# A graph layer's edge loop: folding and adding the group sums later, in own PSUM banks, with the edge attributes copied into PSUM by ScalarE

## The chip, the cores and the metric

The kernel runs on one core of a Trainium2 chip. The time is device microseconds of one launch; a lower one is better.

## The reference

It is a graph layer with 6250 nodes, 206250 edges (sorted by their target `dst`) and 64 features, all in fp32:

```python
h = jnp.maximum(_layernorm(x, axis=-1), 0.0)
msg = jax.nn.relu(h[src] + edge_attr)                      # per edge
agg = jax.ops.segment_sum(msg, dst, num_segments=6250)
z = h + agg
out = x + jax.nn.relu(z @ W1 + b1) @ W2 + b2
```

## The kernel before

**Data.** The edges are taken in groups of 1024, 8 for each of the 128 partitions: 201 full groups and a short one of 4 columns (`NG` is 201, `G` is 8). `z` is kept in SBUF with features on partitions and nodes along the free side. The normalised rows `h` are also written to HBM as `h_rows`, from which edges gather. Groups 0 to 3 (`RAW`) gather from `x` itself and are normalised edge by edge in `norm_edges` (L147 to L157), so that gathers can start before `h_rows` is there.

**Loading.** `load(g)` issues one 256 KB DMA of edge attributes (`ea`) on SyncE's queue and eight gathers (`xg`) on GpSimd's queue (L130), each an indirect DMA of 128 rows. Both tiles have 12 buffers (`LOOK`).

**One group.** `window_sum(g)` builds a one-hot matrix of the edges' targets within a window of 64 nodes on VectorE (`oh`, L294), adds `xg` and `ea` into a PSUM tile `full` (L299, VectorE), and splits the Relu of it into three bf16 parts whose sum is the fp32 value: Relu on ScalarE (L301), the rest on VectorE (L302), its cast on ScalarE (L304), the last rest on VectorE (L305). Eight matmuls (L308) of one-hot and parts add up in the PSUM tile `agg`, 64 targets by three parts.

**Behind it.** `turn(g)` folds the three parts on VectorE (L278) and transposes the sum on TensorE (L280) into PSUM; `sum_into_z(g)` adds it to 64 columns of `z` (L285), at a place that is read from `dst` into VectorE's registers, eight groups at a time (L265). In the loop, group g's `window_sum` is followed by the turn of g-1 and the z add of g-2 (`LAG`).

**Blocks.** When no later group can reach a block of 512 nodes (`READY`), `hidden(c)` multiplies it by W1 (L316) with bias and Relu on ScalarE (L318); one group later `result(c)` multiplies by W2 (L326), adds `x` and `b2` on VectorE (L328) and stores it from SyncE's queue (L330). There are 12 blocks and a short one.

**Once.** Ahead of the loop, the node layernorm (L164 to L200) and `slot`, each edge's place in its window (L219). After group 8, `find_left` checks with three VectorE passes over 128x1612 (L240 to L242), a reduce (L245) and some small ones (L254 to L258) that every edge fell into its window; if one did not, a slow path would follow at the end. After group 9, 13 VectorE adds put b2 into `x_sb` (L353, L355).

The order on each engine is the order of the code: nothing is rescheduled, and engines run ahead of each other as far as buffers and semaphores let them.

Of the kernel before, what the change touches and what calls it, by code (L numbers as in the profile page):

```python
# [9 lines left out]
F32 = mybir.dt.float32  # L10
# [3 lines left out]
ALU = mybir.AluOpType  # L14
# [3 lines left out]
N, E, D = 6250, 206250, 64  # L18
P = 128
G = 8  # L20
GE = P * G
NG = E // GE
# [6 lines left out]
CT = TJ + 1  # L29
W = 64  # L30
WB = 512
R = 4
NB = N // (P * R)
TN = N - NB * P * R
XC = 3
EPS = 1e-5
LOOK = 12
LAG = 2
RV = 8
RAW = 4  # L40
READY = [min(NG, -(-E * P * R * (c + 1) // (N * GE)) + 1) for c in range(NB)]
# [4 lines left out]
def kernel(  # L46
# [14 lines left out]
    nc = tc.nc  # L61
# [5 lines left out]
    work = ctx.enter_context(tc.tile_pool(name="work", bufs=4))  # L67
    dram = ctx.enter_context(tc.tile_pool(name="dram", bufs=1, space=bass.MemoryType.DRAM))
    psum = ctx.enter_context(tc.tile_pool(name="psum", bufs=2, space=bass.MemoryType.PSUM))
# [6 lines left out]
    for c in range(0, NB, XC):  # L76
        nc.sync.dma_start(
            out=x_sb[:, c:c + XC].rearrange("p b r d -> p b (r d)"),
# [55 lines left out]
    def load(g):  # L134
        ea = edge.tile([P, G, D], F32, name="ea")
        attr_load(ea, g)
        xg = edge.tile([P, G, D], F32, name="xg")
        gather(xg, src_sb[:, cols_of(g)], G if g < NG else CT, x if g < RAW else h_rows)
        return ea, xg
# [4 lines left out]
    loaded = [load(g) for g in range(RAW)]  # L144
# [57 lines left out]
    heads, rows = [], []  # L202
# [10 lines left out]

    base = const.tile([1, NG + 1], F32, name="base")
    nc.vector.tensor_copy(base, dst_sb[0:1, 0:C + 1:G])
    pb = psum.tile([P, R * D], F32, name="out", bufs=1)
    nc.tensor.matmul(pb[:, :NG + 1], ones[0:1, :], base, start=True, stop=True)
    slot = const.tile([P, C + CT], F32, name="slot")
    nc.vector.scalar_tensor_tensor(  # L219
# [15 lines left out]

    left = const.tile([P, C + CT], F32, name="left")
    flag = const.tile([1, 1], I32, name="flag")

    def find_left():
        nc.vector.tensor_scalar(left, slot, 1.0, None, op0=ALU.is_lt)  # L240
        nc.vector.scalar_tensor_tensor(left, slot, float(W), left, op0=ALU.is_gt, op1=ALU.add)
        nc.vector.scalar_tensor_tensor(left, dst_sb, 1.0, left, op0=ALU.add, op1=ALU.mult)  # L242
        nc.vector.memset(left[:TD, C + TJ:], 0.0)
        most = const.tile([P, 1], F32, name="most")
        nc.vector.tensor_reduce(most, left, AX.X, ALU.max)  # L245
        pf = psum.tile([P, R * D], F32, name="out", bufs=1)
        nc.tensor.matmul(pf[0:1, 0:1], most, ones[:, 0:1], start=True, stop=True)

        done = const.tile([1, NG + 1], F32, name="done")
        for c in range(-1, NB):  # L250
            to = READY[c + 1] + 1 if c + 1 < NB else NG + 1
            fr = READY[c] + 1 if c >= 0 else 0
            if fr < to:
                nc.vector.memset(done[:, fr:to], float(P * R * (c + 1)))  # L254
        nc.vector.tensor_tensor(done, base, done, ALU.is_lt)
        late = const.tile([1, 1], F32, name="late")
        nc.vector.tensor_reduce(late, done, AX.X, ALU.max)
        nc.vector.tensor_tensor(flag, late, pf[0:1, 0:1], ALU.add)  # L258
# [12 lines left out]
    aggs = {}  # L271

    turned = {}

    def turn(g):
        pa = aggs.pop(g)
        rows = work.tile([W, D], F32, name="agg_rows")
        nc.vector.tensor_reduce(rows, pa.rearrange("w t d -> w d t"), AX.X, ALU.add)  # L278
        pt = psum.tile([D, W], F32, name="turned", bufs=1)
        nc.tensor.transpose(pt, rows, ident[:W, :W])  # L280
        turned[g] = pt

    def sum_into_z(g):
        at = window_start(g)
        nc.vector.tensor_tensor(z[:, ds(at, W)], z[:, ds(at, W)], turned.pop(g), ALU.add)  # L285

    def window_sum(g):
        n = G if g < NG else CT
        cols = cols_of(g)
        ea, xg = loaded[g] if g < RAW else load(g)  # L290
        if g < RAW:
            norm_edges(xg)
        oh = work.tile([P, G, W], BF16, name="oh")
        nc.vector.tensor_tensor(  # L294
            oh[:, :n], slot[:, cols].unsqueeze(2).to_broadcast([P, n, W]),
            wslots.unsqueeze(1).to_broadcast([P, n, W]), ALU.is_equal)

        full = psum.tile([P, G, D], F32, name="full", bufs=2)
        nc.vector.tensor_tensor(full[:, :n], xg[:, :n], ea[:, :n], ALU.add)  # L299
        parts = work.tile([P, G, 3, D], BF16, name="parts")  # L300
        nc.scalar.activation(parts[:, :n, 0, :], full[:, :n], AF.Relu)  # L301
        nc.vector.scalar_tensor_tensor(full[:, :n], full[:, :n], 0.0, parts[:, :n, 0, :],  # L302
                                       op0=ALU.max, op1=ALU.subtract)
        nc.scalar.copy(parts[:, :n, 1, :], full[:, :n])  # L304
        nc.vector.tensor_tensor(parts[:, :n, 2, :], full[:, :n], parts[:, :n, 1, :], ALU.subtract)  # L305
        pa = psum.tile([W, 3, D], F32, name="agg", bufs=2)
        for j in range(n):
            nc.tensor.matmul(pa, oh[:, j, :], parts[:, j], start=(j == 0), stop=(j == n - 1))  # L308
        aggs[g] = pa


    def hidden(c):
        n0 = c * P * R
        p, r = (P, R) if c < NB else (TN, 1)
        p1 = psum.tile([D, P * R], F32, name="big", bufs=1)
        nc.tensor.matmul(p1[:, :p * r], w1_sb, z[:, n0:n0 + p * r], start=True, stop=True)  # L316
        h1 = work.tile([D, R, P], F32, name="h1")
        nc.scalar.activation(h1[:, :r, :p], p1[:, :p * r].rearrange("d (p r) -> d r p", r=r), AF.Relu, bias=b1_sb)  # L318
        return h1

    def result(c, h1):
        n0 = c * P * R
        p, r = (P, R) if c < NB else (TN, 1)
        p2 = psum.tile([P, R * D], F32, name="out", bufs=1)
        for k in range(r):
            nc.tensor.matmul(p2[:p, k * D:(k + 1) * D], h1[:, k, :p], w2_sb, start=True, stop=True)  # L326
        o = work.tile([P, R, D], F32, name="o")
        nc.vector.tensor_tensor(o[:p, :r].rearrange("p r d -> p (r d)"), p2[:p, :r * D],  # L328
                                x_sb[:p, c, :r].rearrange("p r d -> p (r d)"), ALU.add)
        nc.sync.dma_start(out=out[n0:n0 + p * r, :].rearrange("(p r) d -> p (r d)", r=r),  # L330
                          in_=o[:p, :r].rearrange("p r d -> p (r d)"))

    hid = {}

    def blocks_behind(g):
        for c in sorted(hid):
            result(c, hid.pop(c))
        for c in range(NB):
            if READY[c] == g:
                hid[c] = hidden(c)  # L340

    for g in range(NG + 1):
        window_sum(g)
        if g >= 1:
            turn(g - 1)
        if g >= LAG:
            sum_into_z(g - LAG)
            blocks_behind(g - LAG)
        if g == 8:
            find_left()  # L350
        if g == 9:
            for c in range(NB):
                nc.vector.tensor_tensor(x_sb[:, c], x_sb[:, c],  # L353
                                        b2_sb.unsqueeze(1).to_broadcast([P, R, D]), ALU.add)
            nc.vector.tensor_tensor(x_sb[:TN, NB, 0, :], x_sb[:TN, NB, 0, :], b2_sb[:TN], ALU.add)  # L355
    sum_into_z(NG + 1 - LAG)
    blocks_behind(NG + 1 - LAG)
    turn(NG)
    for g in range(NG + 2 - LAG, NG + 1):
        sum_into_z(g)  # L360
        blocks_behind(g)
    hid[NB] = hidden(NB)
    for c in sorted(hid):
        result(c, hid.pop(c))


    def all_windows(msg, lf, n):
# [12 lines left out]
    with tc.If(any_left > 0):  # L380
        with tc.For_i(0, NG, 1) as i:
            idx = work.tile([P, G], I32, name="idx")
            lf = work.tile([P, G], F32, name="lf")
            nc.vector.tensor_copy(idx, src_sb[:, ds(i * G, G)])
            nc.vector.tensor_copy(lf, left[:, ds(i * G, G)])
            ea = edge.tile([P, G, D], F32, name="ea")
            nc.sync.dma_start(out=ea.rearrange("p j d -> p (j d)"),
                              in_=edge_attr[ds(i * GE, GE), :].rearrange("(p j) d -> p (j d)", j=G))
            xg = edge.tile([P, G, D], F32, name="xg")
            gather(xg, idx, G, h_rows)  # L390
            all_windows(combine(xg, ea, G), lf, G)
        ea = edge.tile([P, G, D], F32, name="ea")
        attr_load(ea, NG)
        xg = edge.tile([P, G, D], F32, name="xg")
        gather(xg, src_sb[:, C:], CT, h_rows)
        all_windows(combine(xg, ea, CT), left[:, C:], CT)

        for c in range(NB + 1):
            result(c, hidden(c))


# [37 lines left out]
```

## Time and profile before

| | |
|---|---|
| timed runs, six | median 2051.39 us (2050.29 to 2052.81) |
| profiled execution | 2049.77 us, span 2048.0 us |
| busy share | GpSimd 75%, VectorE 33%, TensorE 20% (weight loads 14%), ScalarE 13% |
| gathers | 1612 (1580 from `h_rows`, 32 from `x`), median 944 ns each, from 4.8 us to 2030.4 us |
| attribute loads | 201 of 256 KB, median 4.8 us from issue to landing |
| the granted TensorE clock | 1.00 in every stage |

In the profile's timeline a line has the start and the length in us, the engine, the line of the kernel, the operation, the tile written and the tiles read (`out<-in`), and, in brackets, how long the engine had been idle and what ended that. In a table by stage a line has the stretch and its length, then for each of PE, PEld (weight loads), DVE (VectorE), ACT (ScalarE) and POOL (GpSimd) the busy time and the number of instructions, then the granted clock, the DMA engines' share and GB/s.

### The profile page before, as it was taken

To read this page: it belongs to the slowest core of one execution; us is meant where nothing else is said; L and a number is where in the kernel's file an instruction comes from. 1 tells how busy PE (TensorE), PEld (TensorE's weight loads), DVE (VectorE), ACT (ScalarE), POOL (GpSimd) and SP (SyncE) were. 2 spreads that over 40 slices of the span, in tenths; PEclk is the share of its full clock that TensorE was granted. 3 is DMA by queue.
4 is the path that set the end of the run, shared out by engine and by line. 5 is a ranking of instruction groups with operands and counts; after the bars stand their busy time and mean duration, and the time that the engine had idled before them with its cause. 6 is when DMAs were issued, how large, how long until landed. Compare 5 with 4: busy or idle time off the path is not lost.

```text
span 2048.0 us, 9645 instructions
## 1 busy us (share of the span) xinstructions
PE 409.7 (20%) x1991; PEld 287.2 (14%) x1991; DVE 670.7 (33%) x1321; ACT 269.2 (13%) x450; POOL 1535.9 (75%) x1619
## 2 busy tenths in 40 slices
PE   2121211211121121122121122112112112112212
PEld 1111111111111111111111111111111111111111
DVE  4662333333323333323333333333233332332332
ACT  3211111111111111111111111111111111111111
POOL 7777777777777777777777777777777777777774
DMA  5211221131131131131122113113113113211311
GB/s 179 62 38 27 84 53 27 44 99 27 26 111 26 26 106 37 27 96 42 27 80 62 27 26 112 26 27 111 32 26 101 37 27 96 47 27 26 104 26 23
DMA packets 87525, 112.95 MB, mean 55 GB/s; under 512 B 30948, under 2 KB 35684, under 8 KB 87460
## 3 DMA queue, kind: packets, MB, share of 16 engines
q0 software_dynamic: 51584, 52.93, 13.5%
q1 hardware_dynamic: 34628, 57.65, 8.3%
q10 hardware_dynamic: 1248, 1.70, 0.2%
q14 instruction: 48, 0.39, 0.1%
q8 instruction: 17, 0.28, 0.1%
HBM read 108.96 MB, written 3.20 MB: 55 GB/s over the span
## 4 chain that ended last, share of the span: by engine, by line
POOL 57%; issue 22%; DMA 17%; DVE 1%; ACT 1%; PE 1%; DVEq 0%; POOLq 0%; ACTq 0%
POOL xg L130 57%; DMA xg<-h_rows,src_sb 17%; PE big L196 0%; ACT z L197 0%; DMA ea<-in_edge_attr_dram 0%; DMA src_sb<-in_src_main_dram 0%; DVE full L302 0%; DVEq L265 0%; DVE x_sb L353 0%; DVE full L299 0%; ACT parts L301 0%; ACT parts L304 0%; DVE parts L305 0%; PE out L326 0%; PE big L316 0%
## 5 line engine op out<-in xcount | busy, mean ns | idle before, releaser
L130 POOL DMA_INDIRECT xg<-h_rows,src_sb x1580 | 1502.1, 951 | 481.5 <-issue 439.1
L308 PE MATMUL agg<-parts,oh 128*64 128x192 bf16 x1612 | 299.8, 367 | 1532.0 <-DVE parts L305 1532.0
L308 PEld LDWEIGHTS <-oh 128*64 128x64 bf16 x1612 | 230.0, 168 | 1586.4 <-DVE parts L305 1568.2
L299 DVE TENSOR_TENSOR full<-xg,ea 128x512 f32<-128x512 f32 x202 | 141.1, 698 | 929.7 <-DMA xg<-h_rows,src_sb 908.8
L301 ACT ACTIVATE parts<-full 128x512 bf16<-128x512 f32 x202 | 120.4, 596 | 1512.5 <-DVE full L299 1510.0
L302 DVE SCALAR_TENSOR_TENSOR full<-full,parts 128x512 f32<-128x512 f32 x202 | 141.1, 699 | 149.7 <-ACT parts L301 149.7
L305 DVE TENSOR_TENSOR parts<-full,parts 128x512 bf16<-128x512 f32 x202 | 139.4, 690 | 131.5 <-ACT parts L304 131.5
L304 ACT CAST parts<-full 128x512 bf16<-128x512 f32 x202 | 118.2, 585 | 154.6 <-DVE full L302 154.6
L294 DVE TENSOR_TENSOR oh<-slot,wslots 128x512 bf16<-128x512 f32 x202 | 135.3, 670 | 0.0
L280 PE MATMUL turned<-ident,agg_rows 64*64 64x64 f32 x202 | 63.1, 312 | 59.8 <-DVE z L285 59.0
L285 DVE TENSOR_TENSOR z<-z,turned 64x64 f32 x202 | 41.1, 203 | 87.6 <-issue 84.5
L278 DVE TENSOR_REDUCE agg_rows<-agg 64x64 f32<-64x192 f32 x202 | 68.4, 338 | 0.0
L280 PEld LDWEIGHTS turned<-ident,agg_rows 64*64 64x64 f32 x202 | 25.5, 126 | 117.4 <-DVE z L285 67.7
L130 POOL DMA_INDIRECT xg<-in_x_dram,src_sb x32 | 32.6, 1019 | 12.4 <-issue 9.4
L316 PE MATMUL big<-z,w_sb 64*64 64x512 f32 (+1 forms) x26 | 24.2, 1032 | 0.3 <-DVE z L285 0.3
L326 PE MATMUL out<-w_sb,h 64*128 64x64 f32 (+1 forms) x98 | 23.6, 418 | 1.2 <-ACT h L318 1.2
L326 PEld LDWEIGHTS out<-w_sb,h 64*128 64x128 f32 (+1 forms) x98 | 22.3, 329 | 3.2 <-ACT h L318 3.2
L196 PE MATMUL big<-ident,ln_h 128*64 128x128 f32 x48 | 12.7, 421 | 33.8 <-DVE ln_h L178 19.1
L328 DVE TENSOR_TENSOR o<-out,x_sb 128x256 f32<-128x256 f32 (+1 forms) x13 | 5.3, 409 | 37.9 <-PE out L326 37.9
L318 ACT ACTIVATE h<-big,b_sb 64x512 f32<-64x512 f32 (+1 forms) x13 | 8.5, 656 | 56.4 <-PE big L316 56.4
L197 ACT COPY z<-big 64x512 f32<-64x512 f32 x12 | 12.6, 1050 | 11.5 <-PE big L196 11.5
L196 PEld LDWEIGHTS big<-ident,ln_h 128*64 128x64 f32 x48 | 6.4, 159 | 39.6 <-issue 19.1
(52 smaller groups left out, 64.0 us busy)
## 6 DMA issues: line engine op xcount, KB each, us to landing
ea<-in_edge_attr_dram SPq DMA_DIRECT2D x201, 256.0 KB, 4.8
xg<-h_rows,src_sb POOLq DMA_INDIRECT x1580, 2.4
x_sb<-in_x_dram SPq DMA_DIRECT2D x4, 384.0 KB, 7.9
h_rows<-ln_h SPq DMA_DIRECT2D x4, 384.0 KB
out_dram<-o SPq DMA_DIRECT2D x12, 128.0 KB, 1.7
dst_sb<-in_dst_main_dram ACTq DMA_DIRECT2D x1, 804.0 KB
src_sb<-in_src_main_dram ACTq DMA_DIRECT2D x1, 788.0 KB
xg<-in_x_dram,src_sb POOLq DMA_INDIRECT x32, 3.0
```

The costliest lines, as they stand in the source:

```text
L130: nc.gpsimd.indirect_dma_start(out=xg[:, j, :], out_offset=None, in_=rows[:, :], in_offset=bass.IndirectOffsetOnAxis(ap=idx[:, j:j + 1], a ...
L278: nc.vector.tensor_reduce(rows, pa.rearrange("w t d -> w d t"), AX.X, ALU.add)
L280: nc.tensor.transpose(pt, rows, ident[:W, :W])
L285: nc.vector.tensor_tensor(z[:, ds(at, W)], z[:, ds(at, W)], turned.pop(g), ALU.add)
L294: nc.vector.tensor_tensor(oh[:, :n], slot[:, cols].unsqueeze(2).to_broadcast([P, n, W]), wslots.unsqueeze(1).to_broadcast([P, n, W]), ALU. ...
L299: nc.vector.tensor_tensor(full[:, :n], xg[:, :n], ea[:, :n], ALU.add)
L301: nc.scalar.activation(parts[:, :n, 0, :], full[:, :n], AF.Relu)
L302: nc.vector.scalar_tensor_tensor(full[:, :n], full[:, :n], 0.0, parts[:, :n, 0, :], op0=ALU.max, op1=ALU.subtract)
L304: nc.scalar.copy(parts[:, :n, 1, :], full[:, :n])
L305: nc.vector.tensor_tensor(parts[:, :n, 2, :], full[:, :n], parts[:, :n, 1, :], ALU.subtract)
L308: nc.tensor.matmul(pa, oh[:, j, :], parts[:, j], start=(j == 0), stop=(j == n - 1))
L326: nc.tensor.matmul(p2[:p, k * D:(k + 1) * D], h1[:, k, :p], w2_sb, start=True, stop=True)
```

## The change

ScalarE copies `ea` into `full`, one group ahead (`take(g+1)` at the head of `window_sum(g)`), and VectorE then adds `xg` to `full` in place. The turn stands two groups behind (`TLAG`), the z add six (`LAG`). `agg` holds two groups in one tile and `turned` four, each with two buffers. The block's products, the start's `pb` and `find_left`'s sum share one tile `big`; `result` and its output add and store are done in separate passes, two and four groups after `hidden`. The small steps at the end of `find_left` move to `judge`, after group 14, and the b2 adds to after group 15.

```diff
-LAG = 2
+LAG = 6
+TLAG = 2
+AB = 2
+TB = 4
...
-    pb = psum.tile([P, R * D], F32, name="out", bufs=1)
+    pb = psum.tile([P, R * D], F32, name="big", bufs=1)
...
+    def judge():
+        pf = found.pop("all")
...
     def turn(g):
         pa = aggs.pop(g)
-        rows = work.tile([W, D], F32, name="agg_rows")
+        rows = work.tile([W, D], F32, name="agg_rows", bufs=LAG)
         nc.vector.tensor_reduce(rows, pa.rearrange("w t d -> w d t"), AX.X, ALU.add)
-        pt = psum.tile([D, W], F32, name="turned", bufs=1)
+        if g % TB == 0:
+            turns.append(psum.tile([D, TB, W], F32, name="turned", bufs=2))
+        pt = turns[-1][:, g % TB]
         nc.tensor.transpose(pt, rows, ident[:W, :W])
         turned[g] = pt
...
+    def take(g):
+
+        n = G if g < NG else CT
+        ea, xg = loaded[g] if g < RAW else load(g)
+        full = psum.tile([P, G, D], F32, name="full", bufs=2)
+        nc.scalar.copy(full[:, :n], ea[:, :n])
+        taken[g] = full, xg
+
     def window_sum(g):
         n = G if g < NG else CT
         cols = cols_of(g)
-        ea, xg = loaded[g] if g < RAW else load(g)
+        if g + 1 <= NG:
+            take(g + 1)
+        full, xg = taken.pop(g)
...
-        full = psum.tile([P, G, D], F32, name="full", bufs=2)
-        nc.vector.tensor_tensor(full[:, :n], xg[:, :n], ea[:, :n], ALU.add)
+        nc.vector.tensor_tensor(full[:, :n], full[:, :n], xg[:, :n], ALU.add)
...
-        pa = psum.tile([W, 3, D], F32, name="agg", bufs=2)
+        if g % AB == 0:
+            banks.append(psum.tile([W, AB, 3, D], F32, name="agg", bufs=2))
+        pa = banks[-1][:, g % AB]
...
     def blocks_behind(g):
+        for c in sorted(res):
+            if READY[c] + 4 <= g:
+                store(c, res.pop(c))
         for c in sorted(hid):
-            result(c, hid.pop(c))
+            if READY[c] + 2 <= g and not res:
+                res[c] = result(c, hid.pop(c))
         for c in range(NB):
             if READY[c] == g:
                 hid[c] = hidden(c)
 
+    take(0)
     for g in range(NG + 1):
         window_sum(g)
-        if g >= 1:
-            turn(g - 1)
+        if g >= TLAG:
+            turn(g - TLAG)
         if g >= LAG:
             sum_into_z(g - LAG)
             blocks_behind(g - LAG)
         if g == 8:
             find_left()
-        if g == 9:
+        if g == 14:
+            judge()
+        if g == 15:
             for c in range(NB):
...
-    sum_into_z(NG + 1 - LAG)
-    blocks_behind(NG + 1 - LAG)
-    turn(NG)
-    for g in range(NG + 2 - LAG, NG + 1):
+    for g in range(NG + 1 - TLAG, NG + 1):
+        turn(g)
+    for g in range(NG + 1 - LAG, NG + 1):
         sum_into_z(g)
         blocks_behind(g)
     hid[NB] = hidden(NB)
+    for c in sorted(res):
+        store(c, res.pop(c))
     for c in sorted(hid):
-        result(c, hid.pop(c))
+        store(c, result(c, hid.pop(c)))
```

More of the change, by code (lines that the diff above doesn't have):

```diff
@@ L237 @@
     flag = const.tile([1, 1], I32, name="flag")
+    found = {}
     def find_left():
@@ L245, in find_left @@
         nc.vector.tensor_reduce(most, left, AX.X, ALU.max)
-        pf = psum.tile([P, R * D], F32, name="out", bufs=1)
+        pf = psum.tile([P, R * D], F32, name="big", bufs=1)
         nc.tensor.matmul(pf[0:1, 0:1], most, ones[:, 0:1], start=True, stop=True)
+        found["all"] = pf
+    def judge():
+        pf = found.pop("all")
         done = const.tile([1, NG + 1], F32, name="done")
@@ L273 @@
     turned = {}
+    banks = []
+    turns = []
     def turn(g):
         pa = aggs.pop(g)
-        rows = work.tile([W, D], F32, name="agg_rows")
+        rows = work.tile([W, D], F32, name="agg_rows", bufs=LAG)
         nc.vector.tensor_reduce(rows, pa.rearrange("w t d -> w d t"), AX.X, ALU.add)
-        pt = psum.tile([D, W], F32, name="turned", bufs=1)
+        if g % TB == 0:
+            turns.append(psum.tile([D, TB, W], F32, name="turned", bufs=2))
+        pt = turns[-1][:, g % TB]
         nc.tensor.transpose(pt, rows, ident[:W, :W])
@@ L285, in sum_into_z @@
         nc.vector.tensor_tensor(z[:, ds(at, W)], z[:, ds(at, W)], turned.pop(g), ALU.add)
+    taken = {}
+    def take(g):
[4 more added lines that the diff above has]
+        taken[g] = full, xg
     def window_sum(g):
@@ L323, in result, with store @@
         p, r = (P, R) if c < NB else (TN, 1)
-        p2 = psum.tile([P, R * D], F32, name="out", bufs=1)
+        p2 = psum.tile([P, R * D], F32, name="big", bufs=1)
         for k in range(r):
             nc.tensor.matmul(p2[:p, k * D:(k + 1) * D], h1[:, k, :p], w2_sb, start=True, stop=True)
+        return p2
+    def store(c, p2):
+        n0 = c * P * R
+        p, r = (P, R) if c < NB else (TN, 1)
         o = work.tile([P, R, D], F32, name="o")
@@ L331, in result @@
                           in_=o[:p, :r].rearrange("p r d -> p (r d)"))
-    hid = {}
+    hid, res = {}, {}
     def blocks_behind(g):
+        for c in sorted(res):
+            if READY[c] + 4 <= g:
+                store(c, res.pop(c))
         for c in sorted(hid):
-            result(c, hid.pop(c))
+            if READY[c] + 2 <= g and not res:
+                res[c] = result(c, hid.pop(c))
         for c in range(NB):
@@ L398 @@
         for c in range(NB + 1):
-            result(c, hidden(c))
+            store(c, result(c, hidden(c)))
 _OUTS = [((N, D), 'float32')]
```

## The prediction

> **What bounds the kernel now.** I read the page first: its busy line, the chain that ended last, and the gather's group.
>
> ```profile
> span 2048.0 us, 9645 instructions
> PE 409.7 (20%) x1991; PEld 287.2 (14%) x1991; DVE 670.7 (33%) x1321; ACT 269.2 (13%) x450; POOL 1535.9 (75%) x1619
> ...
> POOL 57%; issue 22%; DMA 17%; DVE 1%; ACT 1%; PE 1%; DVEq 0%; POOLq 0%; ACTq 0%
> ...
> L130 POOL DMA_INDIRECT xg<-h_rows,src_sb x1580 | 1502.1, 951 | 481.5 <-issue 439.1
> ...
> L299 DVE TENSOR_TENSOR full<-xg,ea 128x512 f32<-128x512 f32 x202 | 141.1, 698 | 929.7 <-DMA xg<-h_rows,src_sb 908.8
> ```
>
> The chain is GpSimd's stream of 1612 gathers, one after the other: 0.94 us of work and 0.30 us between two. VectorE, at its add of L299, waits 909 us for them to land, so ScalarE, TensorE and VectorE have spare time in every group: eight gathers take 10.0 us, and VectorE is a third busy. What the change does to them costs nothing unless it delays GpSimd or the work after the last gather. So I looked at the gather stream alone. In the group of its tile the durations are 940/944/3887 ns (min/median/max): nearly all gathers are alike, and a few are long. The table by stage and the timeline show where those are, and what runs with them.
>
> ```profile
> 46.90:85.00 38.10, 6.27 (x29) 4.45 (x29) 22.71 (x42) 8.19 (x16) 28.83 (x30) 1.00 0.28 75
> 85.00:130.00 45.00, 12.30 (x65) 8.95 (x65) 34.23 (x80) 8.88 (x15) 36.32 (x29) 1.00 0.24 62
> ```
>
> ```profile
> 91.53 0.70 DVE L302 SCALAR_TENSOR_TENSOR full<-full,parts 128x512 f32<-128x512 f32 x1 [0.72 <-ACT parts L301]
> 91.92 0.94 POOL L130 DMA_INDIRECT xg<-h_rows,src_sb  x1 [0.30 <-issue]
> ...
> 98.78 1.58 POOL L130 DMA_INDIRECT xg<-h_rows,src_sb  x1 [0.30 <-issue]
> 98.86 0.68 DVE L299 TENSOR_TENSOR full<-xg,ea 128x512 f32<-128x512 f32 x1
> ...
> 123.76 4.10 DVE L353 TENSOR_TENSOR x_sb<-x_sb,b_sb 128x256 f32<-128x256 f32 x12
> ...
> 124.93 3.89 POOL L130 DMA_INDIRECT xg<-h_rows,src_sb  x1 [0.30 <-issue]
> ```
>
> ```profile
> 1007.24 0.94 POOL L130 DMA_INDIRECT xg<-h_rows,src_sb  x1 [0.30 <-issue]
> 1007.39 0.70 DVE L299 TENSOR_TENSOR full<-xg,ea 128x512 f32<-128x512 f32 x1 [5.45 <-DMA xg<-h_rows,src_sb]
> ```
>
> ```profile
> 419.79 0.70 DVE L299 TENSOR_TENSOR full<-xg,ea 128x512 f32<-128x512 f32 x1 [6.32 <-DMA xg<-h_rows,src_sb]
> 419.98 1.32 POOL L130 DMA_INDIRECT xg<-h_rows,src_sb  x1 [0.30 <-issue]
> ```
>
> In the table the fifth engine column is POOL (busy, and how many). These lines give one pattern. A gather needs something within about 0.1 us of its start; if a VectorE instruction that reads two SBUF tensors is then under way (L299: xg and ea; L353: x_sb and b2), the gather waits until it ends and works for another 0.82 us (99.54 + 0.82 = 100.36 for the one at 98.78; 127.99 + 0.82 = 128.81 for the one at 124.93). Once past that point it is not disturbed: at 1007.39 the add runs inside a gather and both have their usual length. Instructions with one tensor in PSUM and one in SBUF do not disturb it even at that point (L302 from 91.53 across the start at 91.92; nor L294, L305 and L328 wherever they stand).
>
> **The change part by part.** The sum is made against the profiled execution's 2049.77 us (span 2048.0). The six timed runs have a median of 2051.39, which is 1.62 above it.
>
> *The attribute copy and the add.* ScalarE copies ea into PSUM, and the add then reads xg from SBUF and the rest from PSUM, the layout of L302. So its stalls should go. Early, while VectorE catches up, five gathers meet it: those at 90.17, 94.42, 98.78, 103.17 and 107.54 last 1.45, 1.56, 1.58, 1.57 and 1.57 us, 7.73 - 5 x 0.944 = 3.01 too long. Later the adds start just after the sensitive moment (147 of 202 start 0.08 to 0.25 us into a gather), and six gathers are caught: at 419.98, 590.15, 1079.67, 1418.42, 1578.35 and 1910.76, with 1.32, 1.12, 1.37, 1.08, 1.35 and 1.07, together 7.31 - 5.66 = 1.65. **Saved: 4.65 us.**
>
> A page bears on this. The Trainium skill, SBUF — State Buffer, section "Who interferes with whom", says that VectorE with two SBUF inputs contends with a GpSimd instruction that reads SBUF, and that the first to issue holds the ports for its whole length. By its second half the add at 1007.39 would have waited for the gather's end at 1008.18, and then blocked the next gather (due 1008.49) until 1008.88, 0.39 us; over 147 such adds the change would save 57 us. The rows say otherwise, and they decide.
>
> The copy itself is 202 ScalarE instructions of about 0.6 us (bounds 0.59 of L304, 0.63 of the Square of L152, which reads and writes 128x512 in SBUF): 121 us, on an engine idle for 8 of every 10 us. It stands in ScalarE's queue ahead of the previous group's Relu. It waits for VectorE's last subtract of two groups back, hence starts while VectorE does the fold, the z add and the one-hot (1.0 us) and the add (0.7): hidden. If an attribute load were late (each waits on SyncE's queue behind an output store at 12 places, and lands in 4.8 us), Relu and its group would be late by as much; cover is the 5.4 us for which L299 now waits in each group, and beyond it twelve xg buffers, some 120 us of gathers. Zero.
>
> *Fold and turn two behind, z add six behind, in banks of their own; block results split over three passes.* The same 202 folds, transposes, adds and 13 blocks run in a later group; none is waited for by a gather. The out stores move seven groups later on SyncE's queue, where attribute loads stand behind them, with the cover just told. Zero until the tail.
>
> *What moves in time among VectorE's two-SBUF instructions* still costs, by phase. (a) The subtracts and scalings of the first four groups (L150, L157: 8 x 0.69 us) now cost 0.30 + 0.24 at 60.90 and 63.69. The slot step now shares a bank with the last turn and so waits for ScalarE's copy (0.4 us later), and the register load leaves group 2, so they meet other gathers: walked through they cost 0.1 + 0.35 in group 2 and an even chance twice in group 3. I take 0.65, +0.1 (bounds 0 and 2.5). (b) find_left's three passes (111.41 to 116.14) cost 0.90 + 1.32 + 0.63 = 2.85; they move to a similar place: 0 (-0.5 to +0.8 by phase). (c) The 1x202 comparison of L255 costs 0.19 at 118.50; it moves to group 14: -0.15. (d) The b2 adds block from 123.76 to 127.99, 4.23 us, and cost 2.95; any phase gives 2.95 to 4.23. In group 15 they begin where the one-hot now does, 0.18 into a gather, so the next sensitive moment is 1.25 - 0.18 + 0.08 = 1.15 later and the cost 4.23 - 1.15 = 3.08: +0.15.
>
> *Tail.* Before, the last parts end at 2034.43, block 11's first product starts at 2035.51, its result ends at 2040.23, the last o is issued at 2043.31. After, three folds and five z adds come first: last matmul 2035.34, last fold to 2035.74, z adds of groups 196 to 199 one after the other, about 0.26 each, to 2036.7; product 1.96, Relu 0.69, result 1.98, o 0.42, all in one bank, to 2041.9; block 12's product 0.62, Relu 0.35, result 0.63: o at 2043.65, **+0.3** (-0.2 if block 12 needn't wait for o, +0.7 if z adds take 0.36 each).
>
> Sum: -4.65 + 0.1 + 0 - 0.15 + 0.15 + 0.3 = **-4.25**: 2045.5 for a run like the profiled one. The timed runs spread over 2.5 us and lie 1.62 higher; the late stalls depend on landing times by tenths of a microsecond, so I think most of these 1.62 us are more of the same and go too (0 to 1.62; I take 0.9). 2051.39 - 4.25 - 0.9 = **2046.2**.
>
> **The rivals.** *Phases against it:* the mechanism holds, but (a) to (d) and the tail meet their upper bounds (+2, +0.8, 0, +1.3, +0.4 in place of the +0.4 taken) and the timed runs' surplus is something else. Then -4.65 + 4.5: 2051.2, no change; half of it gives 2049. For: each is one fixed phase, not an average. Against: all would have to go one way.
>
> *The add still stalls the gathers, and starts earlier (slower):* reading one operand from PSUM may not be enough, since L302's SBUF operand is bf16 and this one fp32 in 512 columns. Without the ninth wait (ea) the add starts 0.05 us earlier (the chain has 0.05 at VectorE's queue for L299), and each of the 147 adds that comes ahead of a gather's sensitive moment costs up to 0.6 us. From 7 such adds on it is over 4.1 us slower; with 20, 2051.4 + 12 = 2063. For: the margin is a tenth of a microsecond. Against: L328 reads fp32 x_sb beside PSUM and never stretched a gather.
>
> *It changes nothing,* because GpSimd's 0.94 + 0.30 is not touched: then 2051.4. The eleven long gathers speak against it.
>
> **How the numbers follow.** Forecast 0.74, phases against or no effect 0.17, slower 0.09. A measurement of this kernel can tell about 0.2%, 4.1 us, so the line for faster is 2047.3; the forecast, with a range of its own of 2043.8 to 2048.3, passes it about nine times in ten: 0.67 faster. Within 0.2%: 0.07 + 0.15 = 0.22. Slower: 0.11, with a little from phases. The lower end takes the whole surplus, (b) low and no tail cost (2043.8); the upper takes half of the first rival and the surplus kept, 2049.9.
>
> **What would show it right or wrong.** In the changed profile no gather after 200 us should exceed 1.0 us, and in 85 to 130 us only those under find_left. The b2 adds should be over one long gather of 3.8 to 5.1 us near 175 us. The new add should be 0.70 us and ScalarE busy about 390 us. The last gather should start at about 2025 rather than 2029.5. Long gathers beside the new add, or over 15 of them in all, would prove me wrong; so would gathers waiting longer than 0.30 us for a buffer.

## The result and the profile after

| | before | after |
|---|---|---|
| timed runs | median 2050.92 us (2049.42 to 2052.81, 39 runs, the six shown among them) | median 2046.02 us (2043.73 to 2047.14, 19 runs) |
| profiled execution | 2049.77, span 2048.0 | 2045.91, span 2044.1 |

The ratio is 0.9976, with a 95% interval of 0.9969 to 0.9982: faster by 4.9 us. The forecast was 2046.2.

First the page after: the busy line, the gather's group, the new add and the new copy.

```profile
span 2044.1 us, 10215 instructions
...
PE 402.8 (20%) x1991; PEld 294.7 (14%) x1991; DVE 669.4 (33%) x1321; ACT 386.3 (19%) x652; POOL 1531.7 (75%) x1619
...
L133 POOL DMA_INDIRECT xg<-h_rows,src_sb x1580 | 1497.7, 948 | 481.5 <-issue 435.5
...
L322 DVE TENSOR_TENSOR full<-full,xg 128x512 f32<-128x512 f32 x202 | 140.9, 698 | 958.3 <-DMA xg<-h_rows,src_sb 958.3
...
L306 ACT COPY full<-ea 128x512 f32<-128x512 f32 x202 | 118.6, 588 | 199.5 <-DVE parts L328 134.8
```

ScalarE has 117 us more to do, the add takes as long as before, VectorE waits 50 us longer for gathers, and none of that shows in the end. GpSimd is busy 4.2 us less for the same 1612 gathers, and its idle time before a gather is still 481.5 us. The table by stage has the early part of it in GpSimd's column (the fifth): 35 gathers in 34.64 us where 29 took 36.32. Not all of that is won: the long gather of the b2 adds, 3.89 us in this row before, has moved to 177 us.

```profile
85.00:130.00 45.00, 13.62 (x74) 10.29 (x73) 27.83 (x46) 12.75 (x22) 34.64 (x35) 1.00 0.28 72
```

The timeline after, at the places that the prediction was made from:

```profile
109.71 1.59 POOL L133 DMA_INDIRECT xg<-h_rows,src_sb  x1 [0.30 <-issue]
...
110.19 0.98 DVE L244 TENSOR_SCALAR left<-slot 128x1612 f32<-128x1612 f32 x1
111.21 1.84 DVE L245 SCALAR_TENSOR_TENSOR left<-slot,left 128x1612 f32<-128x1612 f32 x1
...
111.60 2.26 POOL L133 DMA_INDIRECT xg<-h_rows,src_sb  x1 [0.30 <-issue]
113.08 1.84 DVE L246 SCALAR_TENSOR_TENSOR left<-dst_sb,left 128x1612 f32<-128x1612 int32 x1
114.17 1.57 POOL L133 DMA_INDIRECT xg<-h_rows,src_sb  x1 [0.30 <-issue]
```

```profile
176.13 4.09 DVE L390 TENSOR_TENSOR x_sb<-x_sb,b_sb 128x256 f32<-128x256 f32 x12
177.29 3.90 POOL L133 DMA_INDIRECT xg<-h_rows,src_sb  x1 [0.30 <-issue]
```

```profile
648.16 0.70 DVE L322 TENSOR_TENSOR full<-full,xg 128x512 f32<-128x512 f32 x1 [8.74 <-DMA xg<-h_rows,src_sb]
648.33 0.94 POOL L133 DMA_INDIRECT xg<-h_rows,src_sb  x1 [0.30 <-issue]
```

find_left and the b2 adds hold the gathers up as before, at other times. The new add, under way across a gather's start at 648.33, does not; the old one did in the same position at 419.79.

To compare the profiles I add up, over all gathers of more than 0.96 us, what each has beyond 0.944 (the columns are the gathers' numbers in order, from 0, and what stands beside the long ones):

| long gathers, us | gathers 0-41: node layernorm | 42-63: edge layernorm of groups 0 to 3 | 64-91 | 92-199 | from 200 on | sum |
|---|---|---|---|---|---|---|
| before | 2.43 | 0.55 | 8.98 (five adds 3.0, find_left 3.0, b2 2.9) | 0 | 1.70 | 13.66 |
| after | 2.66 | 1.34 | 2.58 (find_left) | 3.01 (b2) | 0.02 | 9.62 |
| only the copy | 2.52 | 0.52 | 2.14 (find_left 1.9, b2 0.2) | 2.94 (b2) | 0.00 | 8.12 |
| all but the copy | 2.59 | 2.01 (an add 0.4) | 5.02 | 3.07 | 1.53 | 14.23 |
| copy into SBUF | 2.54 | 1.34 | 4.94 | 0.29 | 4.69 | 13.80 |
| change, b2 in PSUM | 2.19 | 1.35 | 2.56 | 0 | 0.04 | 6.13 |
| the same, find_left through PSUM | 2.50 | 1.36 | 0 | 0 | 0 | 3.86 |
| copy, no two-SBUF instruction | 0.15 | 0 | 0 | 0 | 0.02 | 0.17 |

4.04 us less in long gathers, a first gather 0.20 us earlier and a tail 0.45 us longer (from the last gather's end: 17.57 before, 18.02 after) make 3.79 of the 3.86 us between the two profiled executions.

### The profile page after: what moved, and what is told of

Same layout as the page of the kernel before. It is cut to its first block, busy times and chain, and to the rows that moved or that the text cites. A ratio compares the mean times of both kernels' runs of the same rounds, so it can differ in the third digit from the quotient of the medians.

```text
span 2044.1 us, 10215 instructions
## 1 busy us (share of the span) xinstructions
PE 402.8 (20%) x1991; PEld 294.7 (14%) x1991; DVE 669.4 (33%) x1321; ACT 386.3 (19%) x652; POOL 1531.7 (75%) x1619
## 5 line engine op out<-in xcount | busy, mean ns | idle before, releaser
L133 POOL DMA_INDIRECT xg<-h_rows,src_sb x1580 | 1497.7, 948 | 481.5 <-issue 435.5
L333 PE MATMUL agg<-parts,oh 128*64 128x192 bf16 x1612 | 294.4, 363 | 1593.5 <-DVE parts L328 1593.5
L333 PEld LDWEIGHTS <-oh 128*64 128x64 bf16 x1612 | 237.5, 165 | 1635.1 <-DVE parts L328 778.9
L322 DVE TENSOR_TENSOR full<-full,xg 128x512 f32<-128x512 f32 x202 | 140.9, 698 | 958.3 <-DMA xg<-h_rows,src_sb 958.3
L306 ACT COPY full<-ea 128x512 f32<-128x512 f32 x202 | 118.6, 588 | 199.5 <-DVE parts L328 134.8
L351 PE MATMUL big<-w_sb,h 64*128 64x64 f32 (+1 forms) x98 | 23.6, 418 | 1.2 <-ACT h L343 1.2
L351 PEld LDWEIGHTS big<-w_sb,h 64*128 64x128 f32 (+1 forms) x98 | 22.3, 330 | 3.2 <-ACT h L343 3.2
```

The costliest lines, as they stand in the source:

```text
L133: nc.gpsimd.indirect_dma_start(out=xg[:, j, :], out_offset=None, in_=rows[:, :], in_offset=bass.IndirectOffsetOnAxis(ap=idx[:, j:j + 1], a ...
L306: nc.scalar.copy(full[:, :n], ea[:, :n])
L322: nc.vector.tensor_tensor(full[:, :n], full[:, :n], xg[:, :n], ALU.add)
```

## Experiments: which part of the change does it

The theory is the prediction's: a gather waits if a VectorE instruction with two SBUF inputs is under way at its start, and the copy takes one of those inputs away. The rivals are the rest of the change (the later fold, turn and add, and the banks), and the missing wait on ea.

**All but the copy.**

```diff
-        nc.scalar.copy(full[:, :n], ea[:, :n])
...
-        nc.vector.tensor_tensor(full[:, :n], full[:, :n], xg[:, :n], ALU.add)
+        nc.vector.tensor_tensor(full[:, :n], xg[:, :n], ea[:, :n], ALU.add)
```

> All of the change except ScalarE's copy: the add reads xg and ea from SBUF again. Port theory (a gather waits where a VectorE instruction with two SBUF inputs runs at its start): all the gain goes. Early adds cost about 3.0 us again, later ones 1.65 in a profile and some 1 us more in timed runs, the tail keeps its 0.4: 2050.5 to 2052.5 us, long gathers beside the add. Rival (the gain comes from folding and adding later, or from the banks): stays near 2046.

Measured: 2053.59 us where the kernel before took 2052.66 on that chip, a ratio of 1.0005 (0.9996 to 1.0014). The gain is gone, and the long gathers beside the add are back:

```profile
1148.31 0.70 DVE L321 TENSOR_TENSOR full<-xg,ea 128x512 f32<-128x512 f32 x1 [5.17 <-DMA xg<-h_rows,src_sb]
1148.45 1.37 POOL L133 DMA_INDIRECT xg<-h_rows,src_sb  x1 [0.30 <-DMA xg<-h_rows,src_sb]
```

The forecast's absolute time missed by a microsecond because that chip runs the kernel before 1.7 us slower; only ratios carry over from chip to chip.

**The copy alone.**

```diff
 # in the kernel before; the turn one group behind, the z add two
+    def take(g):
+        n = G if g < NG else CT
+        ea, xg = loaded[g] if g < RAW else load(g)
+        full = psum.tile([P, G, D], F32, name="full", bufs=2)
+        nc.scalar.copy(full[:, :n], ea[:, :n])
+        taken[g] = full, xg
...
-        nc.vector.tensor_tensor(full[:, :n], xg[:, :n], ea[:, :n], ALU.add)
+        nc.vector.tensor_tensor(full[:, :n], full[:, :n], xg[:, :n], ALU.add)
```

> The kernel before with only ScalarE's copy into PSUM and the add in place. Port theory: all the gain comes, without the tail's 0.4 us: 2050.9 - 4.65 - 1 = about 2045.3, between 2044 and 2047. Rival (staging and banks): stays near 2051.

Measured: 2044.19 us, a ratio of 0.9962 (0.9949 to 0.9976); run again on another chip (its expectation is below), 2042.43 us beside 2050.35, again 0.9962 (0.9949 to 0.9976). So the copy brings all of the gain, and the rest of the change brings none. In its profiles no add holds a gather up. They ended at 2044.19 and 2043.53 us, where the whole change's ended at 2045.91: by the table, 1.5 us is in long gathers, most of it in the edge layernorms, which the change moved onto gathers' starts. The intervals of the two ratios overlap (0.9969 to 0.9982 and 0.9949 to 0.9976), so that the staging costs something is likely, and not shown.

**The copy into SBUF.** The add has the waits and the order of the changed kernel, and two SBUF inputs.

```diff
+        eb = work.tile([P, G, D], F32, name="eb", bufs=2)
-        nc.scalar.copy(full[:, :n], ea[:, :n])
+        nc.scalar.copy(eb[:, :n], ea[:, :n])
...
-        nc.vector.tensor_tensor(full[:, :n], full[:, :n], xg[:, :n], ALU.add)
+        nc.vector.tensor_tensor(full[:, :n], eb[:, :n], xg[:, :n], ALU.add)
```

> The changed kernel, but ScalarE copies the attributes into an SBUF tile, so the add has the same waits and order as in the change and two SBUF inputs. Port theory: in the changed kernel 26 adds start up to 0.2 us before a gather and 53 in its first 0.05 us; some 50 of these would now hold a gather up by about 0.6 us each: +30 us, 2060 to 2095. Rival (what helps is that the add no longer waits for ea, or that VectorE's order is looser): stays near 2046.

Measured: 2053.37 us, 1.0006 (0.9997 to 1.0015) of the kernel before. The rival falls: it is where the operand lies that matters. The size was far off, and the reason is in the rows. From 200 us on, 184 adds start a median of 0.05 us after a gather's start. The eight that start 0.21 to 0.05 us ahead of one all hold it up (1.29 to 1.46 us); the fourteen that start 0.044 to 0.003 us ahead hold up none. I had put the moment 0.1 us too late and so counted some 50: the early adds, which follow a one-hot without a pause, stop gathers even when they start up to 0.09 us after them (the add at 98.86 of the kernel before), but nearly all of these late adds start after a wait.

At that moment the other side can lose as well. The 34 late adds that start between 0.044 us before and 0.024 us after a gather's start all end 0.73 us after that start, so that the earliest of them takes 0.77 us in place of 0.70, and the gathers keep their 0.94. In the changed kernel adds in the same place take 0.70. First an add that stops a gather, then one that the gather holds:

```profile
675.58 0.70 DVE L323 TENSOR_TENSOR full<-eb,xg 128x512 f32<-128x512 f32 x1 [5.43 <-DMA xg<-h_rows,src_sb]
675.66 1.43 POOL L133 DMA_INDIRECT xg<-h_rows,src_sb  x1 [0.30 <-issue]
...
1677.36 0.77 DVE L323 TENSOR_TENSOR full<-eb,xg 128x512 f32<-128x512 f32 x1 [5.47 <-DMA xg<-h_rows,src_sb]
1677.40 0.94 POOL L133 DMA_INDIRECT xg<-h_rows,src_sb  x1 [0.30 <-issue]
```

In the changed kernel, six adds start 0.18 to 0.05 us ahead of a gather, and all six gathers take 0.94. In this kernel the b2 adds cost only 0.29 us, so its time flatters it by some 2.7.

**A dose, and its control.** Two more adds in each group, in VectorE's idle time, with both inputs in SBUF or one in PSUM.

```diff
+        if g >= 20:
+            for _ in range(2):
+                idle = work.tile([P, G, D], F32, name="idle", bufs=2)
+                nc.vector.tensor_tensor(idle, xw, yw, ALU.add)   # control: wslots in place of yw
```

> The changed kernel with two more VectorE adds of 128x512 fp32 (0.70 us each, both inputs in SBUF, output unused) after each one-hot from group 20 on, in VectorE's idle time. Port theory: they begin about 0.7 us into a gather and end at 2.1, the next gather's sensitive moment is at 1.33: 0.75 us for each of 182 groups, +136 us (90 to 200), 2136 to 2246. Rival (only VectorE's own queue or the landing matters): within 1 us of 2046, as VectorE has over 5 us idle in each group.

> The control of the dose: the same two added instructions per group, with the second input in PSUM in place of SBUF (one small fill of a constant tile is left over from the other). Port theory: 2046 within 1.5 us, no long gather after group 20. Rival (any VectorE work at that place holds the gathers): as slow as the dose with two SBUF inputs.

Measured, one run each: 2167.07 and 2046.35 us. The dose costs some 120 us, 0.66 for each of 182 groups, though VectorE still waits 5 us for its gathers in each; the control costs nothing. First the dose, then the control:

```profile
1005.83 1.28 DVE L328 TENSOR_TENSOR idle<-slots,yw 128x512 f32<-128x512 f32 x2
1006.38 1.55 POOL L133 DMA_INDIRECT xg<-h_rows,src_sb  x1 [0.30 <-issue]
```

```profile
1008.32 1.27 DVE L328 TENSOR_TENSOR idle<-slots,wslots 128x512 f32<-128x512 f32 x2
1008.85 0.94 POOL L133 DMA_INDIRECT xg<-h_rows,src_sb  x1 [0.31 <-issue]
```

## Experiments: the long gathers that are left

**b2 in PSUM, then find_left too.**

```diff
+    fixed = psum.tile([P, 2, W], F32, name="wslots", bufs=1)
+    wslots = fixed[:, 0]
+    b2_ps = fixed[:, 1]
...
+            nc.vector.tensor_copy(b2_ps, b2_sb)              # the adds then read b2_ps
...
 # the second kernel, in find_left
+        for at in range(0, C + CT, WB):
...
+            nc.scalar.copy(ps[:, :wide], slot[:, at:at + wide])
+            nc.vector.tensor_scalar(part, ps[:, :wide], 1.0, None, op0=ALU.is_lt)
+            nc.vector.scalar_tensor_tensor(part, ps[:, :wide], float(W), part, op0=ALU.is_gt, op1=ALU.add)
...
+            nc.scalar.copy(pd[:, :wide], dst_sb[:, at:at + wide])
+            nc.vector.scalar_tensor_tensor(part, pd[:, :wide], 1.0, part, op0=ALU.add, op1=ALU.mult)
```

> The changed kernel, with b2 copied into PSUM beside the window numbers and the thirteen b2 adds reading it there. Port theory: the gather of 3.90 us at 177.29 becomes 0.94: -3.0 us, about 2043.0 (2042 to 2044). Rival: an add of x_sb still holds it, no change from 2046.

> The same, and find_left's passes done in four parts of 512 columns, each with ScalarE copying slot and dst into PSUM first, so that no VectorE instruction there has two SBUF inputs or runs in its fast form. Port theory: another 2.6 us goes (the gathers at 109.7 to 115.7 us), about 2040.4 (2039.3 to 2041.5); the longer chain of copies delays VectorE by some 5 us in group 8, which twelve gather buffers hide. Rival: that delay reaches the gathers, 2043 or more.

Measured: 2043.05 us (0.9962, 0.9948 to 0.9976) and 2041.41 us (0.9952, 0.9938 to 0.9965). Both lie in the ranges that were given, the second near the upper end: 1.6 us went where 2.6 were expected. In its profile find_left's 2.56 us of long gathers are gone, and the node layernorm's are 0.31 longer. The thirteen b2 adds take as long as before and the gathers run on through them:

```profile
175.91 4.06 DVE L393 TENSOR_TENSOR x_sb<-x_sb,wslots 128x256 f32<-128x256 f32 x12
176.83 0.94 POOL L135 DMA_INDIRECT xg<-h_rows,src_sb  x1 [0.30 <-issue]
178.08 0.94 POOL L135 DMA_INDIRECT xg<-h_rows,src_sb  x1 [0.31 <-issue]
```

**No two-SBUF instruction at all,** on the copy alone: b2 and find_left as above, and the sums and variances of both layernorms in PSUM tiles (`s` and `v` of the node layernorm in buffers of `full`, those of the edge layernorm in `out`).

```diff
-        s = lnp.tile([P, XC * R], F32, name="ln_s")
+        s = psum.tile([P, G, D], F32, name="full", bufs=2).rearrange("p g d -> p (g d)")
...
-        v = lnp.tile([P, XC * R], F32, name="ln_v")
+        v = psum.tile([P, G, D], F32, name="full", bufs=2).rearrange("p g d -> p (g d)")
```

It was first run together with the changed kernel and the copy alone:

> The copy alone (the kernel before plus ScalarE's copy and the add in place), with every other VectorE instruction of two SBUF inputs that meets the gathers also given a PSUM one: b2, find_left in four parts, and the sums and variances of both layernorms. Port theory: of the 8.12 us by which gathers in the profile of the copy alone are too long, all but the first gather's 0.15 go: 2044.2 - 8 = about 2036.2 on that chip (2035 to 2037.5), 0.9925 of the kernel before. Rival (some of these long gathers have another cause, such as loads of x or the first DMAs): 2038 or more.

> The changed kernel, on the same chip as the copy alone: 0.9976 of the kernel before again. It tells whether the staged fold, turn and add cost time beside the copy. By the profiles, long gathers of the first groups sum to 1.5 us more with the staging, and the tail is 0.1 us longer: 1.7 us above the copy alone. Rival (the two are equal and the copy alone met a good chip): within 0.5 us.

> The copy alone once more, as the partner of the run above: 1.7 us under the changed kernel, 0.997 or less of the kernel before. Rival: equal to the changed kernel.

These three runs settled nothing. On that chip engines paused for tens of microseconds (VectorE in the changed kernel for up to 42) without anything in the profile that they waited for, and the kernel before took 2404.09 us, the other three 2439.10, 2430.21 and 2419.56. It shows two things beside. The kernel without two-SBUF instructions had no gather over 0.96 us but the first there either. And the cover of twelve gather buffers, which never mattered elsewhere, is finite: in the changed kernel GpSimd waited 321 us for VectorE.

```profile
POOL xg L133 <- issue: 462.9, 1499, 5.1
POOL xg L133 <- DVE full L322: 321.5, 38, 18.4
```

Why the three were 0.7 to 1.5% slower than the kernel before there stays open. Then again, on a chip without pauses:

> The kernel without two-SBUF instructions once more, because in the run of 2439 us engines paused for tens of microseconds with nothing in the program to wait for, in the kernel before (2404 us) as well. Port theory: gathers after the first all 0.94 us, 0.9925 of the kernel before (0.9915 to 0.9935), some 2036 us where that takes 2051. Rival (some of the long gathers have another cause): above 0.9935.

> The copy alone, once more. From its earlier runs 0.9962 of the kernel before, 0.0036 above the kernel without two-SBUF instructions by 8 us of long gathers. Rival (the copy alone and the whole change are equal, and the earlier five runs were lucky): 0.9976.

Measured: 2036.74 us, a ratio of 0.9932 (0.9919 to 0.9946), and 2042.43 us for the copy alone. This kernel beats both, by 13.6 us against the kernel before. Apart from the first gather nothing is long:

```profile
L132 POOL DMA_INDIRECT xg<-h_rows,src_sb x1580: 940/944/962, 44.8 to 2015.7; - x198
L132 POOL DMA_INDIRECT xg<-in_x_dram,src_sb x32: 940/944/1097, 4.7 to 43.5; - x32
```

So every long gather of the kernel before but the first goes when no VectorE instruction has two SBUF inputs and find_left's first pass, which has one (told of at the end), reads PSUM. Those of the node layernorm are included, which the prediction had left alone.

## Why the prediction was right

The sign and the mechanism held, and so did the size of the main term. That the number met the median to 0.2 us is in part luck: between the profiles 3.86 us went and not 4.25, the surplus of the timed runs shrank by 1.04 and not 0.9, and over 39 runs the kernel before has a median 0.47 us lower than the six runs from which the forecast was counted down.

The ends of the range were worked out wrongly. Both take the 0.9 us of surplus twice: by the terms named, the lower end is 2045.5 - 0.5 - 0.3 = 2044.7 and not 2043.8, the upper 2049.0 and not 2049.9, and no sum leads to the 2048.3 given beside them. The measured 2046.0 lies within the range either way. Step by step:

- **The add's stalls, -4.65.** Right: 3.0 us early and 1.7 us late are gone, and undoing the copy alone brings the gain to nothing. The new add is 0.70 us, the last gather starts at 2025.2, ScalarE is busy 386 us, and in 85 to 130 us only find_left's three gathers are long, all as foretold.
- **What was said to cost nothing** (the copy, the staging, the stores on SyncE's queue): right as far as runs show; GpSimd's idle time is the same 481.5 us. The copy alone being the faster by its profiles suggests that the staging isn't quite free, through (a).
- **(a) Edge layernorms, 0.65 taken:** 1.34. Mis-sized, within the bounds: the walk through had costs in groups 2 and 3 alone. In the profile group 1 costs 0.67 (at 60.94 and 63.88), group 2 as much (at 69.09 and 72.04), and group 3 nothing.
- **(b) find_left, 0:** -0.27, within the bounds. Its first pass has one SBUF input, not two, and is not covered by the pattern as the prediction put it. **(c), -0.15:** -0.19. **(d) b2, +0.15:** 3.01 as against 2.95 before, +0.06. Its lower bound was wrong: "any phase gives 2.95 to 4.23", and in the copy into SBUF it was 0.29.
- **Left out:** the node layernorms' stalls shifted by 0.23, and the first gather came 0.20 earlier.
- **Tail, +0.3:** 0.45, of which 0.28 up to the last `o`, in the order given, z adds 0.25 us apart.

```profile
2031.37 0.94 DVE L297 TENSOR_TENSOR z<-z,turned 64x64 f32 x4
...
2032.37 1.96 PE L341 MATMUL big<-z,w_sb 64*64 64x512 f32 x2 [0.56 <-DVE z L297]
...
2034.37 0.46 DVE L297 TENSOR_TENSOR z<-z,turned 64x64 f32 x2 [2.06 <-PE big L341]
...
2037.11 0.42 DVE L358 TENSOR_TENSOR o<-big,x_sb 128x256 f32<-128x256 f32 x1 [2.28 <-PE big L351]
```

- **The surplus of the timed runs, 0.9 to go:** 1.04 went (2050.92 - 2049.77 = 1.15 before, 0.11 after). But the reason given, that the spread of 2.5 us is late stalls, is not what the runs show: after the change they spread over 3.4 us, as before. With no two-SBUF instruction left five runs spread over 0.8 us, and the copy alone beside them over 3.0, which points to the early instructions; the surplus itself is not settled.
- **The slower rival** had its premise right: the add starts 0.08 us earlier (median 0.146 us after a gather's start before, 0.062 after, from 200 us on). It fails on the operand: none of these adds holds a gather.
- **The page's two halves** (the Trainium skill, SBUF — State Buffer, "Who interferes with whom"): that two SBUF inputs contend with a GpSimd instruction agrees with every run here. That the first to issue holds the ports for its whole length holds for the add: a gather caught at its start waits for the add's end. For the gather it does not: late adds that start over 0.03 us into one take 0.70 us, and the next gather 0.94. Only in the few hundredths of a microsecond around its start does a gather hold an add (the 34 adds of the copy into SBUF).

## What to carry to other kernels

When one engine's stream sets the time, look at the longest of its instructions, not at its mean: here 23 of over 1 us among 1612 alike held all that was won, and what stands beside them in the timeline names the cause. If GpSimd issues indirect DMAs all the time, give each VectorE instruction that meets them one operand in PSUM, early and one-off ones first: 13 b2 adds cost more than all the late adds of the main loop together (2.9 against 1.7 us). Of a change in several parts try the smallest alone; here one copy carried all of the gain.

## What the runs showed of the hardware that I had not expected

The moment at which a late gather is stopped is narrow: in the copy into SBUF, from 200 us on, an add that starts 0.050 us before a gather's recorded start stops it, one that starts 0.044 us before does not. This holds for adds that start after a wait. Of the early adds, which stand directly behind a one-hot, four in the kernel before stopped gathers though they start 0.06 to 0.09 us after them, and one that starts 0.035 us after a gather (at 119.97) did not; where this difference comes from is open. And a row of two-SBUF adds is not always a wall: twelve adds 0.34 us apart held one gather for 2.95 us when it started 0.15 us into an add (2.93 at 0.175, when the copy alone was run again), and let three through with 0.10 us of delay each when they started about 0.19 us into one. In these lines, of the copy into SBUF, the gathers pass between the adds:

```profile
178.39 4.10 DVE L391 TENSOR_TENSOR x_sb<-x_sb,b_sb 128x256 f32<-128x256 f32 x12
179.58 1.04 POOL L133 DMA_INDIRECT xg<-h_rows,src_sb  x1 [0.30 <-issue]
180.93 1.04 POOL L133 DMA_INDIRECT xg<-h_rows,src_sb  x1 [0.31 <-issue]
182.27 1.04 POOL L133 DMA_INDIRECT xg<-h_rows,src_sb  x1 [0.30 <-issue]
```

The one VectorE pass with a single SBUF input that did hold a gather is L244, the first of find_left, 1612 columns in 0.98 us. Where it starts inside a gather it stops it at its end: in the changed kernel the gather of 109.71 was over 0.12 us after that pass, at 111.29. Where it is under way when the gather starts, it stops it there, and 0.82 us of work remain after it, as with two SBUF inputs. So it was in the copy alone (L240 there):

```profile
110.99 0.98 DVE L240 TENSOR_SCALAR left<-slot 128x1612 f32<-128x1612 f32 x1
111.20 1.60 POOL L130 DMA_INDIRECT xg<-h_rows,src_sb  x1 [0.31 <-issue]
```

A row of two-SBUF adds can hold a gather at its end too: the one at 175.98 of the changed kernel, with b2 adds from 0.15 us after its start on, took 1.00 us and was over 0.11 us after the second of them. The Trainium skill has the same figure for such an end: SBUF — State Buffer, "A bandwidth-pool intuition that's wrong", gives VectorE's end plus about 115 ns for a DMA issued by GpSimd that waits for VectorE.
